# Two planner constants, the pace of sixteen scatters and the place of a layer norm's mean factor in a sparse attention layer

## The chip, the cores and the metric

The kernel runs on one core of one Trainium2 chip. Its engines are TensorE (PE, with PEld for its weight loads), VectorE (DVE), ScalarE (ACT), GpSimd (POOL) and the queue of SyncE (SP). Times are device microseconds (us) of that core; less is better.

## The reference

One layer of a graph network on 4096 nodes of width 512, with 8 heads of 64:

```python
hs = layer_norm(x);  ht = layer_norm(h_target)
q = (ht @ Wq + bq) / sqrt(64);  k = hs @ Wk + bk;  v = hs @ Wv + bv
logits = where(adj != 0, q . k per head, -1e30)
ctx = softmax(logits) @ v
ht = ht + ctx @ Wo + bo
ht = layer_norm(ht)
out = layernorm(x + ht + gelu(ht @ W1) @ W2)
```

`adj` is 4096 x 4096 and sparse: some 17 neighbours to a row, the row itself among them. All is in float32.

## The kernel before, in words

**Two programs in one.** `adj_resnorm_kernel` treats each row by the list of its neighbours. A flag tells at the end whether a list was longer than planned; only then does the dense `general_path` run, which it does not here.

**Lists.** Rows come in 32 tiles of 128. For each tile `edges` loads the adjacency rows, takes the sign on ACT (L733), and on DVE multiplies by a column count (L740) and draws the largest column numbers (L742, L749 to L766). Tiles 0 to 15 are part one, 16 to 31 are part two. `sort(part)` then ranks the rows of a part by degree on DVE and PE (L819 to L867), and POOL writes the 16 record tiles of the part to DRAM in ranked order, one indirect DMA each (L871); these are called the sort's scatters below. Part one's lists, its sort and seven of part two's tiles are done beside the projections, in the first 280 us. Nine tiles of part two and the second sort are left for the stage after.

**Attention by lists.** Ranked rows are taken in groups of two tiles (the first and the last group have one): first seven groups and a half of part one, from short lists to long, then part two from long to short. A tile has as many slots as its longest list, and slots are taken three at a time, here called a *triple*; there are 211. For a triple POOL gathers three rows of keys and values per target row into a ring of 17, later 20, slots (L985); DVE multiplies by the query (L1239), sums per head (L1244), multiplies values by the exponentials (L1200) and adds some slots (L1204, L1207); ACT takes the exponentials (L1248, L1257) and scales the third slot (L1220, L1223); PE adds up the slots by transposes into PSUM (L1211). `front` makes a tile's query: gather, scale, transposes (L1021), the product with Wq on PE (L1031) and its move out of PSUM on DVE (L1036), without which the tile's first L1239 can't start.

**After a tile.** `finish` divides (L1101 to L1122), multiplies by Wo (L1128, L1132), copies to `h` (L1137) and takes moments (L697). Once per group it then does the second layer norm: DVE shifts the variance (`n_ve`, L680), POOL raises it to the power -1/2 (`n_rs`, L687), DVE makes the mean factor (`n_nm`, L692), ACT applies both (L1150), PE transposes `h` (L1159) and ACT moves the result out as `h2T` (L1163). `finish` is advanced one step at every half group, that is twice per triple.

**Feed-forward.** `feed(g)` can start when `h2T` of group g stands. It goes in pairs: eight blocks of products with W1 (L1344) and their GELU (L1347), and, one block later, the products with W2 (L1353) into `po`. `end` then adds x (L1300), takes the sums (L1302, L1305), shifts (L1309), has POOL raise to the power (L687 again), makes the mean factor (L1314), applies both (L1317), and POOL writes the rows out (L1321). It is advanced one step with each block of the next group's feed.

**What sets the order.** `_weave` interleaves four streams by costs in the planner's own units: attention and feed are given 60 units to a group of two tiles each, the rest of the lists starts at `WAIT` units, and weights are loaded beside them. Every engine executes in order. The framework's scheduler takes the woven program, may put an instruction ahead of others whose inputs it expects later, and fixes each engine's order when the program is built. L1159, L1031, L1021, L1117, L1132 and the sort's matmuls share two PSUM buffers named `t`, so a product into `t` waits until the tile before the last one was read.

```python
            def other_lists():
                for cost in ed:
                    yield 2.2 * cost
                keep_rest()
                yield from sort(1)
            _weave((att, 0), (chain(feed(g) for g in range(len(GROUPS))), 0), (other_lists(), WAIT),
                   (weights(), 0))
```

Of the kernel before, what the change touches and what calls it, by code (L numbers as in the profile page):

```python
# [443 lines left out]
def adj_resnorm_kernel(  # L444
# [56 lines left out]
    NA, NBT = len(CAPS_A), len(CAPS_B)  # L501
# [31 lines left out]
    with tc.tile_pool(name="keep", bufs=1) as keep:  # L533
# [17 lines left out]
        with ExitStack() as late:  # L551
# [22 lines left out]
            def turn_of(name, places):  # L574
                turns[name] += 1
                return places[turns[name] % len(places)]
# [106 lines left out]
            def power(pool, mv, n, name, ve=None):  # L683
                if ve is None:
                    ve = shifted(pool, mv, n, name)
                rs = pool.tile([P, n], F32, name=name + "_rs")
                nc.gpsimd.tensor_tensor(rs, ve, mhalf[:, :n], ALU.pow)  # L687
                return rs

            def negmean(pool, mv, rs, n, name):  # L690
                nm = pool.tile([P, n], F32, name=name + "_nm")
                nc.vector.scalar_tensor_tensor(nm, mv[:, :, 0], -1.0, rs, op0=ALU.mult, op1=ALU.mult)  # L692
                return nm
# [23 lines left out]
            def behind(ins):  # L717
                return tc.issue_after(ins[-1]) if ins else nullcontext()
# [51 lines left out]
            def keep_rest():  # L770

                while held:
                    nc.sync.dma_start(*held.pop())
# [40 lines left out]
            def sort(part):  # L814

                i0, n = PARTS[part]
                me = slice(i0, i0 + n)
                pool, R = lp, Rs[part]
                nc.vector.tensor_reduce(deg[:, me], dpart[:, me, :], AX.X, ALU.add)  # L819
                nc.vector.tensor_copy(R[:, :, DEG], deg[:, me])  # L820
                dif, rank = tools[:, 928:928 + n], tools[:, 944:944 + n]
                ranki, b16 = tools[:, 960:960 + n].bitcast(I32), tools[:, 976:984].bitcast(BF16)
                nc.vector.scalar_tensor_tensor(dif, deg[:, me], float(RE), cnt[:, me], op0=ALU.min,
                                               op1=ALU.not_equal)
                nc.vector.tensor_reduce(bad[:, 1 + part:2 + part], dif, AX.X, ALU.max)
                nc.vector.tensor_scalar(dif, deg[:, me], 0.0, float(NB - 1), op0=ALU.max,
                                        op1=ALU.min)
                nc.vector.tensor_scalar(b16, dif, -1.0, float(NB - 1), op0=ALU.mult, op1=ALU.add)
                if part:
                    oh = turn_of("wide", wide).bitcast(BF16)  # L830
                else:
                    oh = wp.tile([P, NB * n], BF16, name="oh")
                oh = oh[:, :NB * n].rearrange("p (b i) -> p b i", b=NB)
                nc.vector.tensor_tensor(oh, b16.unsqueeze(1).to_broadcast([P, NB, n]),
                                        bins.unsqueeze(2).to_broadcast([P, NB, n]), ALU.is_equal)
                ohf = oh.rearrange("p b i -> p (b i)")
                pos = turn_of("wide", wide).bitcast(F32)
                pos = pos[:, :NB * n].rearrange("p (b i) -> p b i", b=NB)
                posf = pos.rearrange("p b i -> p (b i)")
                w = NB * n // 2  # L840
                yield 6.0 if part else 2.0
                tots = []
                for c in range(2):
                    sl = slice(c * w, (c + 1) * w)
                    pt = ps.tile([P, w], F32, name="t" if part else "cps", bufs=2)
                    nc.tensor.matmul(pt, ones_bf, ohf[:, sl], start=True, stop=True)
                    tots.append((sl, pt))
                if not part:
                    yield 6.0
                for c, (sl, pt) in enumerate(tots):  # L850
                    with behind([] if part else maxima):
                        scan = nc.vector.tensor_tensor_scan(
                            posf[:, sl], one_c.to_broadcast([P, w]), pt,
                            0.0 if c == 0 else posf[:, c * w - 1:c * w],
                            op0=ALU.mult, op1=ALU.add)
                while factors:
                    with behind([scan.ins]):
                        factors.pop()()
                yield 4.0
                for c in range(2):  # L860
                    sl = slice(c * w, (c + 1) * w)
                    pa = ps.tile([P, w], F32, name="t" if part else "cps", bufs=2)
                    nc.tensor.matmul(pa, lower, ohf[:, sl], start=True, stop=True)
                    nc.vector.tensor_add(posf[:, sl], pa, posf[:, sl])
                nc.vector.tensor_mul(pos, pos, oh)
                nc.vector.tensor_reduce(rank, pos.rearrange("p b i -> p i b"), AX.X, ALU.add)
                nc.vector.tensor_copy(ranki, rank)  # L867
                yield 10.0
                for i in range(n):
                    with behind(issues):  # L870
                        ins = nc.gpsimd.indirect_dma_start(  # L871
                            out=recs_d[part][:, :],
                            out_offset=bass.IndirectOffsetOnAxis(ap=ranki[:, i:i + 1], axis=0),
                            in_=R[:, i, :], in_offset=None)

                    tc.declare_no_dep(ins.ins, group=f"scatter{part}", reason="other rows")
                    tc.add_to_no_dep_group(f"scatter{part}", ins.ins)
                    yield 3.0 if part else 1.3
                done.add(part)


# [213 lines left out]
            def finish(i, p, cps, group, hs, mv):  # L1095
# [48 lines left out]
                ve = shifted(sp, mv[:, :nh, :], nh, "n2")  # L1144
                yield
                rs = power(sp, mv[:, :nh, :], nh, "n2", ve)
                yield
                nm = negmean(sp, mv[:, :nh, :], rs, nh, "n2")
                for j, h in enumerate(hs):
                    nc.scalar.activation(h, h, AF.Identity, bias=nm[:, j:j + 1], scale=rs[:, j:j + 1])  # L1150
# [144 lines left out]
            def end(group, xs, po):  # L1295

                nt = len(group)
                sm = sp.tile([P, 2, 2], F32, name="sm3")
                for j in range(nt):
                    nc.vector.scalar_tensor_tensor(xs[j], xs[j], 1.0, po[j], op0=ALU.mult,  # L1300
                                                   op1=ALU.add, accum_out=sm[:, j, 0:1])
                nc.vector.tensor_scalar_mul(sm[:, :nt, 0], sm[:, :nt, 0], -1.0 / D)  # L1302
                yield
                for j in range(nt):
                    nc.scalar.activation(po[j], xs[j], AF.Square, bias=sm[:, j, 0:1],  # L1305
                                         accum_out=sm[:, j, 1:2])
                yield
                ve = sp.tile([P, nt], F32, name="n3_ve")
                nc.vector.tensor_scalar(ve, sm[:, :nt, 1], 1.0 / D, EPS, op0=ALU.mult, op1=ALU.add)  # L1309
                yield  # L1310
                rs = power(sp, None, nt, "n3", ve)
                yield
                nm = sp.tile([P, nt], F32, name="n3_nm")
                nc.vector.tensor_mul(nm, sm[:, :nt, 0], rs)  # L1314
                yield
                for j in range(nt):
                    nc.scalar.activation(xs[j], xs[j], AF.Identity, bias=nm[:, j:j + 1],  # L1317
                                         scale=rs[:, j:j + 1])
                yield
                for j, i in enumerate(group):  # L1320
                    ins = nc.gpsimd.indirect_dma_start(  # L1321
                        out=out[:, :], out_offset=bass.IndirectOffsetOnAxis(
                            ap=tags[:, i, TGT:TGT + 1], axis=0),
                        in_=xs[j], in_offset=None)

                    tc.declare_no_dep(ins.ins, group="out", reason="other rows")
                    tc.add_to_no_dep_group("out", ins.ins)
# [68 lines left out]
            def chain(gens):  # L1396
                for g in gens:
                    yield from g

            WAIT = 100.0  # L1400
            AHEAD = 4
            ADDS = 11
            HEAVY = 30
# [68 lines left out]

            def other_lists():
                for cost in ed:
                    yield 2.2 * cost
                keep_rest()
                yield from sort(1)

            _weave((att, 0), (chain(feed(g) for g in range(len(GROUPS))), 0), (other_lists(), WAIT),
                   (weights(), 0))  # L1480

# [34 lines left out]
```

## Time and profile before

| | |
|---|---|
| three runs | 1788.15, 1792.07, 1799.92 us; median 1792.07 |
| the profiled execution | 1783.65 us, its span 1781.9 us, 22,463 instructions |
| PE busy | 1666.0 us (93%), clock granted 0.971 on average |
| DVE busy | 1425.0 us (80%) |
| ACT busy | 1240.4 us (70%) |
| POOL busy | 1018.9 us (57%) |
| first L1239 of attention | 282.3 us; last one 1656.4 us |
| last nine tiles' signs (L733) | about 383 to 708 us |
| second sort's scatters (L871) | 768 to 852 us |

The page gives busy time by engine over the whole span and in 40 slices of 44.5 us. Since stages have different limits, the waits, the stretches by window and the engines' instructions in order of time are read with it. A window's row has busy time and number of instructions for PE, PEld, DVE, ACT and POOL, then the clock that TensorE was granted, the share of the DMA engines and GB/s. A row of the waits tells who waited, for whom, the total, how often, and the longest. In a row in order of time the bracket at the end holds the idle time before it and what ended that.

### The profile page before, as it was taken

Reading aid. Unit: us, or ns where it says so; the run is one execution under the profiler, and the core shown is the slowest. Engines: PE = TensorE matmul, PEld = TensorE weight load, DVE = VectorE, ACT = ScalarE, POOL = GpSimd, SP = SyncE. Lnnn points to the kernel's source line nnn. Section 1 sums busy time; section 2 is a strip of 40 time slices with the busy share of each in tenths; the row PEclk is TensorE's granted clock in tenths of the full one; section 3 lists DMA queues with packets and bytes.
Section 4 is the critical chain, followed back from the end, with each engine's and each line's share of the span. In section 5 each row is a group of like instructions: output and inputs, shape, how many; then the busy total and the mean of one; then the engine's idle time right before and its main releaser. Section 6 shows DMA issues by size and latency. Waiting matters only on the chain. (4 is left out here: it accounts for less than half of the span.)

```text
span 1781.9 us, 22463 instructions
## 1 busy us (share of the span) xinstructions
PE 1666.0 (93%) x6850; PEld 1078.9 (61%) x6850; DVE 1425.0 (80%) x2449; ACT 1240.4 (70%) x3133; POOL 1018.9 (57%) x822
## 2 busy tenths in 40 slices
PE   7999994889999999997989999999999999999997
PEld 3444443656666776665657667666666666666665
DVE  6887787868788989996989898989897888988500
ACT  5876673648777888675777877787776777877511
POOL 1000146655557566778886787777677767764101
PEclk9999997899999999998999999999999999999998
DMA  9999988877778797867888788877667777675000
GB/s 353 383 388 367 344 272 324 318 249 270 250 241 308 273 322 268 271 204 232 285 298 284 274 282 294 295 259 260 234 218 269 249 235 239 233 260 194 21 4 26
DMA packets 141610, 461.00 MB, mean 259 GB/s; under 512 B 18036, under 2 KB 23048, under 8 KB 141480
## 3 DMA queue, kind: packets, MB, share of 16 engines
q0 software_dynamic: 96272, 342.33, 56.7%
q1 hardware_dynamic: 37392, 94.06, 14.9%
q10 hardware_dynamic: 7816, 23.08, 3.3%
q8 instruction: 57, 0.93, 0.2%
q14 instruction: 73, 0.60, 0.1%
HBM read 430.61 MB, written 28.79 MB: 258 GB/s over the span
## 5 line engine op out<-in xcount | busy, mean ns | idle before, releaser
L985 POOL DMA_INDIRECT kv<-kvd,rec x603 | 795.4, 1319 | 335.4 <-issue 118.5
L1344 PE MATMUL pf<-h2T,w 128*128 128x256 f32 (+1 forms) x2176 | 474.5, 372 | 4.5 <-ACT h2T L1163 4.5
L1353 PE MATMUL po<-w,gt 128*128 128x512 f32 x1024 | 463.7, 594 | 0.0
L1344 PEld LDWEIGHTS pf<-h2T,w 128*128 128x128 f32 x2176 | 393.0, 193 | 74.3 <-issue 20.3
L1239 DVE TENSOR_TENSOR kv<-kv,tq 128x1536 f32<-128x1536 f32 (+2 forms) x211 | 351.1, 1675 | 55.6 <-DMA kv<-kvd,rec 52.0
L1223 ACT ACTIVATE kv<-kv,pa 128x64 f32<-128x64 f32 x1520 | 390.9, 336 | 4.4
L1244 DVE TENSOR_REDUCE lg<-kv 128x24 f32<-128x1536 f32 (+2 forms) x211 | 350.0, 1667 | 0.6
L1353 PEld LDWEIGHTS po<-w,gt 128*128 128x128 f32 x1024 | 187.6, 191 | 194.5 <-issue 193.1
L1211 PEld LDWEIGHTS cps<-ident,kv 128*128 128x128 f32 x1828 | 217.6, 144 | 121.5 <-issue 41.8
L1211 PE MATMUL cps<-ident,kv 128*128 128x128 f32 x1828 | 244.1, 280 | 50.1 <-DVE kv L1200 32.1
L1200 DVE TENSOR_TENSOR kv<-kv,p 128x1024 f32<-128x1024 f32 (+1 forms) x211 | 251.1, 1192 | 25.8 <-ACT p L1248 24.4
L687 POOL TENSOR_TENSOR n_rs<-n_ve,mhalf 128x2 f32<-128x2 f32 (+2 forms) x51 | 53.4, 1047 | 327.4 <-DVE n_ve L680 133.0
L733 ACT ACTIVATE kv<-kv 128x1024 uint8<-128x1024 int32 x128 | 134.4, 1052 | 53.4 <-DMA kv<-in_adj_dram 21.8
L1347 ACT ACTIVATE gt<-pf 128x512 f32<-128x512 f32 x128 | 76.4, 597 | 100.9 <-PE pf L1344 97.4
L1347 ACT ACT_TABLE_LOAD x110 | 141.1, 1283 | 1.8
L1132 PE MATMUL t<-wo,rb 128*128 128x512 f32 x256 | 121.0, 615 | 8.1 <-DVE rb L1122 8.1
L947 PE MATMUL pq<-wv,h2T 128*128 128x512 f32 x256 | 117.0, 600 | 3.3 <-DVE rbc L662 2.4
L947 PE MATMUL pq<-wk,h2T 128*128 128x512 f32 x256 | 119.1, 608 | 1.0 <-DVE h2T L928 1.0
L1031 PE MATMUL t<-wq,tq 128*128 128x512 f32 x256 | 116.8, 600 | 1.3 <-ACT tq L1024 1.3
L742 DVE MAX8 cand<-kv 128x8 uint16<-128x171 uint16 (+1 forms) x384 | 108.2, 324 | 1.2
L1248 ACT ACTIVATE p<-lg 128x24 f32<-128x24 f32 (+2 forms) x179 | 38.9, 218 | 75.3 <-DVE lg L1244 73.9
L947 PEld LDWEIGHTS pq<-wv,h2T 128*128 128x128 f32 x256 | 48.9, 193 | 66.8 <-issue 57.5
(163 smaller groups left out, 1586.0 us busy)
## 6 DMA issues: line engine op xcount, KB each, us to landing
kv<-in_adj_dram SPq DMA_DIRECT2D x128, 512.0 KB, 7.3
kvd<-tq ACTq DMA_DIRECT2D x23, 512.0 KB, 6.9
kv<-kvd,rec POOLq DMA_INDIRECT x603, 6.0
kv<-in_L_gnn_h_target_dram SPq DMA_DIRECT2D x32, 256.0 KB, 6.3
kv<-in_x_dram SPq DMA_DIRECT2D x15, 512.0 KB, 8.5
kvd<-kv ACTq DMA_DIRECT2D x9, 512.0 KB, 6.5
w<-in_L_gnn_W_dram SPq DMA_DIRECT2D x4, 1024.0 KB, 8.2
w<-in_L_gnn_W_dram ACTq DMA_DIRECT2D x4, 1024.0 KB, 14.1
```

The source lines that it names most:

```text
L733: nc.scalar.activation(sg, a, AF.Sign, accum_out=dpart[:, i, h:h + 1])
L947: nc.tensor.matmul(pkv, hT[:, kc, j * P:(j + 1) * P], w[:, kc, :], start=kc == 0, stop=kc == KC - 1)
L985: issues[:] = [nc.gpsimd.indirect_dma_start(out=dst, out_offset=None, in_=table[:, :], in_offset=bass.IndirectOffsetOnAxis(ap=idx, axis=0) ...
L1132: nc.tensor.matmul(pa, ct[:, c, :], wo[:, c, :], start=False, stop=c == KC - 1, skip_group_check=True)
L1200: nc.vector.tensor_tensor(v4, v4, p[:, j0:j0 + m, :].unsqueeze(3) .to_broadcast([P, m, H, HD]), ALU.mult)
L1211: nc.tensor.matmul(cps[:, c, :], kv[:, j, D + c * P:D + (c + 1) * P], ident, is_transpose=True, start=j0 + j == 0 and c == 0, stop=j0 + n ...
L1223: newest[:] = [nc.scalar.mul(v, v, pa[:, hd:hd + 1]).ins]
L1239: nc.vector.tensor_tensor(kv[:, :n, :D], kv[:, :n, :D], tq[:, :D].unsqueeze(1).to_broadcast([P, n, D]), ALU.mult)
L1244: logits[:] = [nc.vector.tensor_reduce(lg[:, :n, :], kv[:, :n, :D].rearrange("p j (h d) -> p j h d", h=H), AX.X, ALU.add).ins]
L1344: nc.tensor.matmul(pf[:, k, :], w1[(f0 + k) // KC][:, kc, (f0 + k) % KC * P:((f0 + k) % KC + 1) * P], h2T[:, kc, :w], start=kc == 0, stop= ...
L1347: nc.scalar.activation(gt, pf, AF.Gelu_apprx_tanh)
L1353: nc.tensor.matmul(po[j], gt[:, k, j * P:(j + 1) * P], w2[(f0 + k) // KC][:, (f0 + k) % KC, :], start=False, stop=f0 + k == FC - 1, skip_g ...
```

## The change

Four edits. The rest of part two's lists starts at 140 planner units in place of 100, and each of its steps is given 1.6 times its cost in place of 2.2, so that the stream ends at 312.8 units in place of 337.6. The sixteen scatters of the second sort are 4.5 units apart in place of 3.0 (332.8 to 404.8 in place of 357.6 to 405.6). In `finish`, for groups that end in a tile of part two, four steps in place of one lie between POOL's power and DVE's mean factor. In `end` one more step lies between the two.

```diff
@@ sort
-                    yield 3.0 if part else 1.3
+                    yield 4.5 if part else 1.3
@@ finish
                 rs = power(sp, mv[:, :nh, :], nh, "n2", ve)
-                yield
+                for _ in range(1 if i < NA else 4):
+                    yield
                 nm = negmean(sp, mv[:, :nh, :], rs, nh, "n2")
@@ end
                 rs = power(sp, None, nt, "n3", ve)
                 yield
+                yield
                 nm = sp.tile([P, nt], F32, name="n3_nm")
@@ adj_resnorm_kernel
-            WAIT = 100.0
+            WAIT = 140.0
+            PACE = 1.6
@@ other_lists
                 for cost in ed:
-                    yield 2.2 * cost
+                    yield PACE * cost
```

## The prediction

> **What bounds the kernel now.** I read the page, the stretches by window, the waits, and then the engines in order of time around each gap of TensorE. First the page:
>
> ```profile
> span 1781.9 us, 22463 instructions
> PE 1666.0 (93%) x6850; PEld 1078.9 (61%) x6850; DVE 1425.0 (80%) x2449; ACT 1240.4 (70%) x3133; POOL 1018.9 (57%) x822
> PEclk9999997899999999998999999999999999999998
> ```
>
> PE is busy nearly throughout, at full clock save for a few slices. The stretches tell which of them have another limit (columns: PE, PEld, DVE, ACT, POOL, clock, DMA share, GB/s):
>
> ```profile
> 443.00:719.00 276.00, 271.21 (x1230) 187.44 (x1229) 234.14 (x412) 216.63 (x544) 170.34 (x137) 0.99 0.79 275
> 811.00:870.00 59.00, 46.54 (x195) 32.03 (x194) 42.70 (x44) 33.84 (x92) 47.75 (x39) 0.88 0.76 246
> 1340.00:1360.00 20.00, 15.81 (x71) 12.33 (x70) 15.48 (x22) 12.56 (x28) 12.32 (x11) 0.83 0.75 261
> 1665.00:1782.00 117.00, 104.99 (x444) 69.91 (x442) 13.13 (x75) 24.75 (x47) 11.29 (x13) 0.96 0.06 19
> ```
>
> From 443 to 719 us, where most of the lists lie, PE lacks 4.8 us in 276. After 1665 us attention is over and PE works off the feed alone. So PE's work is fixed, nothing stands behind it at the end but the last group's output, and the end moves by what PE's gaps and its slow clock cost before. The waits say who makes the gaps:
>
> ```profile
> PE cps L1211 <- DVE kv L1200: 32.1, 8, 6.6
> PE cps L1211 <- DVE kv L1204: 17.7, 9, 12.5
> PE t L1159 <- DVE tq L1036: 8.3, 2, 4.2
> DVE n_nm L692 <- POOL n_rs L687: 40.1, 27, 7.8
> ```
>
> The third and fourth row belong together. This is PE, and then DVE, at the border of two groups of part two:
>
> ```profile
> 1342.32 0.60 PE L1159 MATMUL t<-ident,h 128*128 128x128 f32 x4
> 1347.11 1.12 PE L1159 MATMUL t<-ident,h 128*128 128x128 f32 x4 [4.19 <-DVE tq L1036]
> ...
> 1348.58 5.65 PE L1344 MATMUL pf<-h2T,w 128*128 128x256 f32 x16
> ...
> 1354.28 3.62 PE L1344 MATMUL pf<-h2T,w 128*128 128x256 f32 x16
> ```
>
> ```profile
> 1339.84 0.16 DVE L692 SCALAR_TENSOR_TENSOR n_nm<-mv,n_rs 128x2 f32<-128x2 f32 x1 [7.84 <-POOL n_rs L687]
> ...
> 1344.28 0.17 DVE L1309 TENSOR_SCALAR n_ve<-sm 128x2 f32<-128x2 f32 x1 [1.58 <-ACT po L1305]
> 1346.29 0.16 DVE L1314 TENSOR_TENSOR n_nm<-sm,n_rs 128x2 f32<-128x2 f32 x1 [1.84 <-POOL n_rs L687]
> 1346.37 0.68 DVE L1036 SCALAR_TENSOR_TENSOR tq<-t,bqr 128x512 f32<-128x512 f32 x1
> ```
>
> DVE waits three times in a row, for both norms, before it reads the query out of a `t` buffer that the transposes of `h` need. PE has no feed left, idles 4.19 us, and its next 16 matmuls take 5.65 us where 3.62 is usual: the half clock after a gap.
>
> **Norm's mean factor, part two.** Four such borders cost PE. At 1067.6 us: gaps 2.65 and 0.38, then 8 matmuls in 5.29 for 3.60, in all 4.7. At 1257.8: gap 4.06, then 1.11 for 0.60 and 5.85 for 3.62, 6.8. At 1347.1: 4.19, 0.52 and 2.03, 6.7. At 1600.4: gap 2.25, then 22 matmuls in 6.32 for 4.98 and 0.37 on four transposes, 4.0. Sum 22.2 us.
>
> The Trainium skill ("TensorE: Matmul & The Clock Gate", Part 1) has the array fall to half clock after an idle window of some 3.4 us. By it the two gaps of 2.65 and 2.25 us would cost nothing more than themselves and the sum would be some 19 us; these rows show the slow matmuls after them too, and the rows stand.
>
> The order of the built programs shows what the edit really moves. L692 itself stays right behind its shift on DVE in nearly every group of part two, as before, so the 4 to 8 us that DVE waits for POOL mostly remain. What moves is the feed: `h2T` is announced three half groups later, feed starts at 612.6 units in place of 605.5 in the tenth group, and runs 7 units, one pair of blocks, behind from there. So at 1257 and 1347 PE gets two more blocks with W2 (3.44 us each) ahead of the transposes of `h`, at 1067 one, at 1600 one of each kind; and DVE's L1300 to L1314 go behind L1036 at 1257 and 1347. The filler of 6.9 us covers 4.06 and 4.19, that of 3.44 covers 2.65. I cost the delay of the feed itself at nothing: feed only slips into the 117 us at the end, where PE has no lack of it. If the filler came too early, the gaps would return whole. Taken: -22, from -26 (the 0.3 to 0.9 us gaps near them go too) to 0.
>
> **Scatters apart.** The second limit is POOL:
>
> ```profile
> 765.29 0.96 POOL L985 DMA_INDIRECT kv<-kvd,rec  x1 [2.18 <-PE cps L1211]
> ```
>
> ```profile
> 823.03 1.76 DVE L1239 TENSOR_TENSOR kv<-kv,tq 128x1536 f32<-128x1536 f32 x1 [10.63 <-DMA kv<-kvd,rec]
> ```
>
> ```profile
> 834.75 1.97 PE L1211 MATMUL cps<-ident,kv 128*128 128x128 f32 x8 [12.46 <-DVE kv L1204]
> ...
> 933.37 2.82 PE L1211 MATMUL cps<-ident,kv 128*128 128x128 f32 x12 [6.56 <-DVE kv L1200]
> ```
>
> After 765.29 POOL waits for nobody until 940.8 us; an instruction starts 0.30 us after the last ended. DVE waits 10.63 us for triple 78, and PE idles 12.46 and later 6.56. A scatter takes POOL 1.0 us and 0.3. I counted POOL's instructions in the built orders. Up to the last gather of triple 78 the changed kernel has 12 scatters and two output writes in front, before 10 and none: four more, 4 x 1.3 = 5.2 us. Against it stand the wait of 2.18 at 765, and 2.8 that POOL waited at 717 to 720 for two outputs and a rest list, which now stand 7 triples earlier. So triple 78 comes at about the same time, and **the big gap stays**. Behind it, up to triple 95, four instructions fewer: -5.2 us, which the gap at 933 (6.56, and 1.35 by 12 transposes in 2.82 for 1.47) can take. Taken: -5, from -20 (both gaps and their clock) to +6 (L687 and an output, now side by side behind triple 57, hold POOL while DVE makes both norms).
>
> **Lists later and closer.** The work is the same: per tile four L740 of 0.41 us, twelve L742 of 0.32 and some 2.6 us of decoding, about 8 us on DVE. By the two orders and the rows' means, DVE's work falls from 67.0 to 55.8 us in triples 14 to 23, and rises from 237.5 to 255.5 in triples 24 to 61. In that stretch PE's own work is 261 us, and DVE waited for PE 10.1, 6.3 and 4.7 us at L1036 of tiles 6 to 8: room for 21 of the 18 us more, but not in the same tiles. Tiles 9 to 11 have 133.9 us of DVE work (before 126.0) against 134.0 of PE, and tile 10 now ends like the border shown above, with L1300 to L1314 ahead of L1036: at most another 7. The adjacency goes along on SP's queue: 36 loads of 512 KB, 7.3 us each to landing, were 58 GB/s over the 325 us of signs and are 80 over the 236 that 172.8 units in place of 237.6 leave; at 275 GB/s and 0.79 in the window that makes some 0.85 of the DMA engines. ACT's signs move with it, to an engine busy 217 us of 276. Both at nothing, beside gathers that land before DVE asks; gathers late by it are within the upper end. Taken +5, from -3 to +18. In triples 16 to 18 the lists go away from DVE, but the order also puts L692 two triples later there: the gaps at 394 to 407 (9.0 us) become, instruction by instruction, 1.4 us longer; from -6 to +4. The sort's sums (L864) held PE 3.07 us at 752; now they stand ahead of L1036 of tile 11 with three blocks of other matmuls between. Taken -2, from -5 to +3.
>
> The skill ("SBUF — State Buffer", on the port pair that VectorE and GpSimd share) says that a two-input DVE instruction and a GpSimd one exclude each other, which speaks against closer lists. Here a gather at 811.07 took 2.16 us beside L1239 and 0.94 at 813.53 without; the L740s are as many as before and short, so no term comes of it.
>
> The extra step in `end` changes the order of L1314 by a triple at most, and is in the counts above: 0.
>
> **Sum.** -22 - 5 + 5 + 1.4 - 2 = -22.6 us on the profiled 1783.65 (span 1781.9 and 1.75 around it): 1761. The median of the runs shown is 8.4 above that execution; for the median I take 1792.07 - 22.6 = **1770**.
>
> **Rivals.**
> - *The fillers don't fill.* L692 stays where it was, and another wait ends in the same place, say ACT's h2T (L1163), for which PE waited 0.7 us after L1159 at 775. Then only -5 + 4.4 remains: 1791. For it: DVE's waits at L692 remain. Against: two blocks are 6.9 us.
> - *POOL is freed as well.* If spreading lets POOL keep its lead of some 20 us (gather's end to L1239 at triples 69 to 72), the gap of 12.46 and its slow 2.5 go too: 1770 - 15 = 1755. For it: POOL waited for ring slots up to 765. Against: the count.
> - *Slower: PE runs dry at every border.* If on the chip `h2T` really comes three half groups later in each of the nine last groups, each loses 3 x 2.8 us (102.4 us of a group over 36 half groups) less 6.9 of filler and adds one half-clock window of 1.7: 3.2 x 9 = 29, none of the 22 is won, and 1792 - 5 + 29 + 4 = 1820. It decides where L692 stands more than one triple behind L680 on DVE. The built order has it within one.
>
> **Chances.** Forecast, 1760 to 1781: 0.56. Fillers fail or the lists eat the gain, 1781 to 1800: 0.25. POOL freed, under 1760: 0.11. Slower, about 1820: 0.08. The range leaves out the last, and half of what lies beyond its other end: 1750 to 1796. Within 1% of 1792 (1774 to 1810), about what a measurement of this kernel can tell from no change, lie the second case and a third of the first's upper part: faster 0.57, same 0.35, slower 0.08.
>
> **What would show it.** L1159 after the changed borders without a wait for L1036; L1344 at 3.6 us for 16 there; L692 still waiting 4 to 8 us; POOL without waits from triple 66 on, a gap of 10 us or so at triple 78, none of 6 at triple 93; new waits of PE on L1200 near triples 50 to 58. Wrong if PE's gaps elsewhere grow: each new one of 4 us costs 6 to 7.

## The result: a little slower, and the profile after

The changed kernel takes 1797.52 us (median of 16 runs, 1790.22 to 1802.30), the kernel before 1790.47 (16 runs): a ratio of 1.0036, 95% interval 1.0021 to 1.0050, some 6.4 us more. The forecast was 22.6 us less, in a range that ended at 1796.

```profile
span 1798.9 us, 22449 instructions
PE 1669.7 (93%) x6850; PEld 1077.0 (60%) x6850; DVE 1422.3 (79%) x2449; ACT 1232.7 (69%) x3127; POOL 1010.9 (56%) x822
PEclk9999998898999999999999999999999999999999
```

The page gives DVE, ACT and POOL a few us less work than before, and PE the same matmuls in 3.7 us more. Most of the time went into PE's idle time (115.9 us of the span before, 129.2 now). The profiled execution (1800.67 us, span 1798.9) is a slow one among the 16, and that of before (1783.65) a quick one among its 16. A part of their difference has nothing to do with the change: up to the first L1239 of attention every engine has the same instructions in the same order, and this stage took 282.3 us there and 290.3 here (285.1 to 290.8 in fifteen of the sixteen profiles taken later). So I compare from that L1239 on, by stretches between the first L1239 of certain triples:

```
triples                     0-23    24-61   62-109   110-210  after 210    sum
before                     161.1    275.7    301.0     636.3     125.5   1499.6
changed                    162.1    288.6    298.5     627.4     132.0   1508.6
difference                  +1.0    +12.9     -2.5      -8.9      +6.5     +9.0
```

PE's work is the same, some 1605 us by the count of matmuls at 3.43 us for sixteen of L1344. What it idles, and what its busy time holds above that rate, is 131.3 us from the first L1239 on before and 140.9 now. By stretches of triples 0 to 23, 24 to 47, 48 to 76, 77 to 109 and from 110 on, it was 51.3, 5.9, 9.8, 29.2 and 35.1; now it is 52.5, 2.7, **30.5**, 21.8 and **33.5**. The first bold figure is the loss. The second is the gain of 22 us that did not come.

The waits tell of both (total, times, longest):

```profile
DVE n_nm L692 <- issue: 22.2, 5, 5.4
DVE n_nm L692 <- POOL n_rs L687: 20.1, 20, 4.1
PE pf L1346 <- ACT h2T L1164: 13.5, 9, 4.2
PE t L1160 <- DVE tq L1036: 1.3, 1, 1.3
```

L692 waits in total as long as before (42.3 us; 40.1 before). The wait of the transposes of `h` for L1036 fell from 8.3 us to 1.3, as forecast. But the first product of the next group (L1346, which is L1344 before) now waits 13.5 us for `h2T`, where it waited 4.5; behind triple 110 it is 9.1 for 0.4.

This is PE, and then ACT, at the border whose gap of 4.19 us the prediction showed:

```profile
1352.55 3.60 PE L1355 MATMUL po<-w,gt 128*128 128x512 f32 x8
1355.98 0.60 PE L1212 MATMUL cps<-ident,kv 128*128 128x128 f32 x4
1356.42 3.60 PE L1355 MATMUL po<-w,gt 128*128 128x512 f32 x8
1359.86 1.04 PE L1160 MATMUL t<-ident,h 128*128 128x128 f32 x8
1365.12 7.04 PE L1346 MATMUL pf<-h2T,w 128*128 128x256 f32 x18 [4.23 <-ACT h2T L1164]
```

```profile
1360.87 1.28 ACT L1258 ACT_TABLE_LOAD   x1 [8.37 <-DVE lg L1245]
...
1362.62 2.00 ACT L1224 ACTIVATE kv<-kv,pa 128x64 f32<-128x64 f32 x8
1364.53 1.90 ACT L1164 ACTIVATE h2T<-t,cols 128x256 f32<-128x256 f32 x4
```

Both blocks with W2 now stand ahead of the transposes and cover the wait for L1036. Nothing stands behind the transposes. ACT moves `h2T` out only after the exponentials and eight L1224 of two triples, and PE idles 4.23 us and runs on at half clock (18 products in 7.04 us, of which sixteen take 3.62 elsewhere), as before, one instruction later. The same happens at 1093.56 (3.50 us) and, shorter, at 1278.13 (1.13). (From L1148 on the changed kernel's lines are one to three higher than before: L1160 is L1159 there, L1212 is L1211, L1346 is L1344. Kernels with the steps of the norm alone, as norm2 below, have them one higher throughout.)

Now the stretch that lost, while DVE is at triples 47 to 51. First POOL, then DVE, then PE, in order of time:

```profile
631.58 0.58 POOL L998 DMA_DIRECT2D rec<-rec  x1 [6.03 <-DVE p L1101]
635.06 1.02 POOL L1323 DMA_INDIRECT out_dram<-xt,tags  x1 [2.89 <-ACT xt L1319]
...
652.46 1.14 POOL L985 DMA_INDIRECT xt<-in_x_dram,tags  x1 [6.21 <-DMA out_dram<-xt,tags]
```

```profile
664.96 1.76 DVE L1240 TENSOR_TENSOR kv<-kv,tq 128x1536 f32<-128x1536 f32 x1 [9.65 <-issue]
```

```profile
670.00 1.11 PE L1021 MATMUL t<-ident,tq 128*128 128x128 f32 x4 [4.76 <-ACT tq L1017]
673.34 6.05 PE L1355 MATMUL po<-w,gt 128*128 128x512 f32 x8 [2.23 <-ACT gt L1349]
```

POOL stands at a record load, at an output write, and at a gather of x whose buffer that write still reads. The gathers of keys queue behind, DVE waits 9.65 us, and PE idles 4.76 and 2.23 us, for a scaled query and for a GELU. The profile names nothing for DVE's wait here ("issue"); I take it for the gather, since in the kernel with the list edit alone the same wait is put down to it:

```profile
663.62 1.76 DVE L1239 TENSOR_TENSOR kv<-kv,tq 128x1536 f32<-128x1536 f32 x1 [8.70 <-DMA kv<-kvd,rec]
```

### The profile page after: what moved, and what is told of

The parts are those of the page before. It is cut to its first block, busy times and chain, and to the rows that moved or that the text cites. A ratio compares the mean times of both kernels' runs of the same rounds, so it can differ in the third digit from the quotient of the medians.

```text
span 1798.9 us, 22449 instructions
## 1 busy us (share of the span) xinstructions
PE 1669.7 (93%) x6850; PEld 1077.0 (60%) x6850; DVE 1422.3 (79%) x2449; ACT 1232.7 (69%) x3127; POOL 1010.9 (56%) x822
## 5 line engine op out<-in xcount | busy, mean ns | idle before, releaser
L1346 PE MATMUL pf<-h2T,w 128*128 128x256 f32 (+1 forms) x2176 | 478.7, 374 | 13.5 <-ACT h2T L1164 13.5
L1346 PEld LDWEIGHTS pf<-h2T,w 128*128 128x128 f32 x2176 | 394.6, 195 | 82.4 <-issue 19.0
L1224 ACT ACTIVATE kv<-kv,pa 128x64 f32<-128x64 f32 x1520 | 390.7, 336 | 4.1
L1212 PEld LDWEIGHTS cps<-ident,kv 128*128 128x128 f32 x1828 | 215.3, 143 | 118.0 <-issue 52.9
L1212 PE MATMUL cps<-ident,kv 128*128 128x128 f32 x1828 | 244.3, 279 | 44.8 <-DVE kv L1201 16.6
L687 POOL TENSOR_TENSOR n_rs<-n_ve,mhalf 128x2 f32<-128x2 f32 (+2 forms) x51 | 43.6, 854 | 332.3 <-DVE n_ve L680 139.0
L1132 PE MATMUL t<-wo,rb 128*128 128x512 f32 x256 | 117.4, 601 | 4.8 <-DVE rb L1122 4.8
L1031 PE MATMUL t<-wq,tq 128*128 128x512 f32 x256 | 117.3, 601 | 1.5 <-ACT tq L1024 0.9
```

The source lines that it names most:

```text
L1132: nc.tensor.matmul(pa, ct[:, c, :], wo[:, c, :], start=False, stop=c == KC - 1, skip_group_check=True)
L1212: nc.tensor.matmul(cps[:, c, :], kv[:, j, D + c * P:D + (c + 1) * P], ident, is_transpose=True, start=j0 + j == 0 and c == 0, stop=j0 + n ...
L1224: newest[:] = [nc.scalar.mul(v, v, pa[:, hd:hd + 1]).ins]
L1346: nc.tensor.matmul(pf[:, k, :], w1[(f0 + k) // KC][:, kc, (f0 + k) % KC * P:((f0 + k) % KC + 1) * P], h2T[:, kc, :w], start=kc == 0, stop= ...
```

## The experiments

All times are medians in us against the kernel before on the same chip, of 6 to 12 executions each and 21 to 33 of the kernel before. "Steps" are those between POOL's power and DVE's mean factor.

| run | edit | time | before | ratio, 95% interval |
|---|---|---|---|---|
| norm4 | before + four steps | 1802.09 | 1792.28 | 1.0055, 1.0032 to 1.0078 |
| lists | before + WAIT 140, PACE 1.6 | 1805.43 | 1792.28 | 1.0079, 1.0053 to 1.0105 |
| lists_scatter | lists + scatters 4.5 apart | 1798.99 | 1792.28 | 1.0038, 1.0018 to 1.0058 |
| endstep | before + the step in `end` | 1795.58 | 1792.28 | 1.0024, 0.9998 to 1.0050 |
| x_later | changed, x gathered two blocks later | 1803.71 | 1795.76 | 1.0033, 1.0012 to 1.0053 |
| closer | before + PACE 1.6, scatters 4.5 apart | 1802.84 | 1795.76 | 1.0044, 1.0020 to 1.0068 |
| no_norm | changed without the four steps | 1804.49 | 1795.76 | 1.0035, 1.0011 to 1.0059 |
| before_x_later | before, x gathered two blocks later | 1803.15 | 1795.76 | 1.0044, 1.0019 to 1.0070 |
| after_recs | changed + eight record buffers | 1795.84 | 1792.43 | 1.0027, 1.0006 to 1.0049 |
| after_free | after_recs + x later + first scatter later | 1801.01 | 1792.43 | 1.0057, 1.0034 to 1.0080 |
| before_recs | before + eight record buffers | 1782.80 | 1792.43 | 0.9947, 0.9926 to 0.9969 |
| norm2 | before + two steps | 1783.15 | 1792.43 | 0.9938, 0.9916 to 0.9960 |
| norm3 | before + three steps | 1785.21 | 1790.35 | 0.9974, 0.9958 to 0.9990 |
| after_norm2 | changed with two steps for four | 1787.39 | 1790.35 | 0.9984, 0.9966 to 1.0002 |
| norm2_recs | before + two steps + eight buffers | 1775.24 | 1790.35 | 0.9916, 0.9896 to 0.9936 |
| scatter2 | before, scatters 2.0 apart | 1788.65 | 1790.35 | 0.9988, 0.9971 to 1.0004 |

Each kernel has one profile. A single profile may lie several us off its kernel's median, so I rest on a stretch only where several kernels with the same edit agree in it.

### Each part alone

```diff
# norm4
-                yield
+                for _ in range(1 if i < NA else 4):
+                    yield
# lists
-            WAIT = 100.0
+            WAIT = 140.0
+            PACE = 1.6
-                    yield 2.2 * cost
+                    yield PACE * cost
# lists_scatter: lists, and
-                    yield 3.0 if part else 1.3
+                    yield 4.5 if part else 1.3
# endstep: in end, behind power
+                yield
```

The scatters could not be spread alone: 4.5 apart behind the old end of the lists, they come later than the planner needs their records.

> Only the four steps between POOL's power and DVE's mean factor in part two; lists, scatters and end as before. Theory 'lists lose' (the changed kernel's extra 7 us come from the list edit between triples 48 and 77, and the norm edit only trades PE's wait for L1036 at the borders for a wait of the next group's first W1 block for ACT's h2T): -4 to +2 us, with PE's gaps at the borders of triples 110, 141 and 154 ended by h2T, and the idle and slow time of PE after triple 110 within 5 us of the 33.5 of before. Rival 'norm loses' (feed runs 7 units late and its last 7 us come out behind attention as they are): +5 to +9 us. The prediction's term: -22 us, that idle and slow time falls to some 12 us.

> Only WAIT 140 and PACE 1.6; scatters at 3.0, norm and end as before. Theory 'lists lose': +10 to +18 us, and the idle and slow time of PE between triples 48 and 77 rises from 9.8 us to 25 to 30, with POOL standing 4 to 6 us at a gather of x that waits for an output write to land, and DVE then 8 to 10 us at an L1239. Rival 'norm loses': within 3 us of before. The prediction's term: +4 us for lists and sort sums together, up to +18 at the end of its range.

> The list edit and the scatters at 4.5 units; norm and end as before. Theory 'lists lose': 5 to 10 us less than the list edit alone, since in the changed kernel PE's idle and slow time from triple 77 to 93 was 9.4 us and before 18.2; so +3 to +10 us against before, near the changed kernel's +7. Rival 'norm loses': -8 to 0 us against before. The prediction's term: -5 for the scatters.

> Only the extra step in end. Both theories and the prediction: within 2 us of before. A third, 'end loses': the extra step puts the output write next to the gather of x on POOL, which waits for it and holds the gathers of keys behind it: +5 to +10 us, and a stop of POOL of some 6 us at a gather of x is seen here (in the built order one such place stands behind the group of triple 36, where before four gathers lie between write and gather of x) and not with the list edit alone.

**norm4** lost 9.9 us, more than either theory gave it. PE's idle and slow time behind triple 110 was 47.1 us. No gap there is ended by L1036 any more; in their place stand L1345 for `h2T` (4.06 us), L1212 for L1205 (3.42 and 3.33) and L1031 for ACT (3.73). At 1430, near triple 173, POOL's power came behind seven gathers that started after its input stood, and DVE stood still at L692:

```profile
1430.04 0.16 DVE L692 SCALAR_TENSOR_TENSOR n_nm<-mv,n_rs 128x2 f32<-128x2 f32 x1 [8.85 <-issue]
```

**lists** lost 13 to 14 us, and everything that "lists lose" said of it came: 28.9 us in triples 48 to 76, POOL 5.8 us at the gather of x, DVE 8.70 us at an L1239. **lists_scatter** gave back about 7 us by time, give or take 6. **endstep** gave no clear verdict, its interval reaching from below 0 to +9 us; POOL stood at gathers of x for 3.7, 2.3 and 5.4 us there, and one of 6 was not seen. Added up the parts would give more than 20 us, and the changed kernel has 6.4. The parts do not add.

### Is it the write, the lateness or the closeness?

```diff
# x_later (changed kernel), before_x_later (kernel before)
-                    if f0 == FC // 2:
+                    if f0 == 12:
# closer: lists_scatter with
-            WAIT = 140.0
+            WAIT = 100.0
```

> The changed kernel, with each group's gathers of x asked for at f0 = 12 in place of 8 (two blocks of W1 later), so that on POOL they no longer stand right behind the output writes whose buffer they need. Theory 'write wait' (in the list edit POOL stands 5.8 to 6.2 us at a gather of x until an output write has landed, holds the gathers of keys of triple 59 behind it, DVE idles 9 us and PE 6 to 7 and its clock falls): 8 to 11 us less than the changed kernel, 1787 to 1790; idle and slow time of PE in triples 48 to 61 from 18.5 to under 9. Rival 'close lists' (DVE's 18 us more of list work in triples 24 to 61 make attention late there, and the gather is only what DVE meets last): within 3 us of the changed kernel, 1795 to 1800, and triples 48 to 61 stay above 14.

> The kernel before with PACE 1.6 and scatters at 4.5, but WAIT 100 as before: lists closer, not later; they end at 272.8 units, 65 earlier than before. Theory 'write wait': the gathers of x stand 7 to 10 instructions behind the writes in the lists' groups here, so the stop of 6 us is gone and triples 48 to 76 stay under 18 us of idle and slow time; with scatters done sooner the gap of 12.5 us at triple 78 shrinks: -12 to -2 us against before. Rival 'close lists': DVE has more list work per triple from triple 18 to 45 than before, +5 to +15 us, idle and slow time in triples 14 to 47 above 30 us where before has 21.

> The changed kernel without the four steps of the norm (lists, scatters and the step in end stay). Theory 'parts add': 10 us less than the changed kernel, since the norm edit alone cost 9.9: 1787. Rival 'order' (what the norm edit does at each border hangs on where the built order has the neighbours, and in the changed kernel idle and slow time after triple 110 is 33.5 us, as before, though the norm edit alone has 47.1): within 3 us of the changed kernel. The prediction's term: 22 us more than the changed kernel.

> The kernel before with only the gathers of x asked for two blocks later. It measures what the write wait cost there: POOL waited 1.7 us at 540 and 4.9 at 1209 at a gather of x, with no gap of PE behind either. Theory 'write wait': within 4 us of before, either way. Rival: another place of 34 gathers moves the built order as much as any edit here did, +5 to +12 us.

**x_later** took POOL's stop of 6.2 us away (a gather of x now stands 7.3 us at 453, and PE's idle and slow time in triples 24 to 47 is 3.8 us), and with it the gap at 670, but no time. Triples 48 to 61 kept 20.3 us: PE now idled at 732, behind the sort's sums on DVE.

```profile
732.39 2.07 PE L1031 MATMUL t<-wq,tq 128*128 128x512 f32 x2 [6.72 <-DVE kv L864]
```

So the write wait was only what DVE met last, and the theory that priced it at 8 to 11 us fell. **before_x_later** showed beside this that moving those gathers costs 8 us by itself in the kernel before, which makes x_later a blunt test; after_free below repeats it, the same move included, with other holds gone. By the numbers set down beforehand, 'close lists' came in x_later (within 3 us of the changed kernel, over 14 us in triples 48 to 61).

**closer** met neither theory in full. It lost 7.9 us, as its rival said, though triples 14 to 47 had only 17.7 us of idle and slow time; triples 48 to 76 kept 27.8, and 42.8 came behind 110, where the lists are long done. Its use is in the next reading: DVE's work in triples 24 to 61, in one window each of the kernel before, the changed one, closer and after_free (the columns are those of the prediction's windows: the length, then PE, PEld, DVE and so on):

```profile
443.40:719.20 275.80, 271.01 (x1229) 187.31 (x1228) 233.91 (x412) 216.50 (x543) 170.54 (x137) 0.99 0.79 275
```

```profile
452.40:741.00 288.60, 276.74 (x1234) 189.22 (x1233) 248.48 (x473) 227.10 (x555) 166.90 (x139) 0.98 0.78 273
```

```profile
452.60:731.20 278.60, 266.99 (x1203) 185.03 (x1202) 234.36 (x402) 216.27 (x537) 174.42 (x144) 0.98 0.77 263
```

```profile
447.10:735.50 288.40, 274.95 (x1234) 188.31 (x1233) 248.72 (x474) 226.70 (x555) 167.12 (x138) 0.99 0.78 275
```

The reader is to see two pairs. With 234 us of DVE work the stretch takes 276 and 279 us, with 248.5 it takes 288 and 289. The eight other profiles without WAIT 140 have 271 to 282 us here, and the six other kernels with it, however the rest was changed, 287 to 291. DVE's idle time is 40 to 44 us in all four. Its makeup is not the same: before, 21.1 of it were waits for PE, 10.6 for gathers and 6.4 for ACT; changed, 9.4, 17.9 (the 9.65 shown above among them) and 9.6. What differs between the two groups of kernels is WAIT and with it DVE's work in the stretch; that the work is the cause is how I read the pairs, and no run adds work there by itself.

**no_norm** stands where the changed kernel does (1.0035 and 1.0036). The four steps, which lose 10 us alone, neither gain nor lose by time within the changed kernel, give or take 5 us. That is what "order" said. The two profiles are less alike than the times: behind triple 110 no_norm has some 44 us of idle and slow time where the changed kernel has 33.5, and in the stretches to triple 76 it has 6 less. One profile of each doesn't tell which of this is the edit's.

### Take POOL's holds away

```diff
# after_recs (changed kernel), before_recs (kernel before)
-                rec = sp.tile([P, E0 + MAXE], I32, name="rec", bufs=6)
+                rec = sp.tile([P, E0 + MAXE], I32, name="rec", bufs=8)
# after_free: after_recs, x_later, and ahead of the scatters
-                yield 10.0
+                yield 18.0 if part else 10.0
-                    yield 4.5 if part else 1.3
+                    yield 4.0 if part else 1.3
```

> The changed kernel with eight buffers for the records in place of six, so that POOL's load of the next record (L998) no longer waits for DVE's L1101 to have read an old one. Theory 'POOL held' (with the lists closer POOL stands 13 us at L998 between triples 48 and 62, 9 at an output write and a gather of x, and 8 at the first scatter, loses its lead of ring slots, and enters the stretch from triple 62 to 109, where its 184 instructions take 300 us whatever the scatters do, that much later): 4 to 10 us less than the changed kernel, 1788 to 1794; POOL's waits for DVE in triples 48 to 61 from 16.4 us to under 6. Rival 'next wait' (the wait only passes to the next thing, the gather of x, the scatter or DVE's own lists): within 3 us of the changed kernel, with triples 48 to 76 still above 26 us of idle and slow time.

> The changed kernel with all three holds of POOL taken away: eight record buffers, the gathers of x asked for two blocks later, and the first scatter 8 units further behind the sort, with 4.0 in place of 4.5 units between scatters, so that the last is as late as before. Theory 'POOL held': 8 to 14 us less than the changed kernel, 1784 to 1790, idle and slow time in triples 48 to 76 from 30.5 to under 18. Rival 'next wait': within 4 us of the changed kernel, and POOL or DVE wait elsewhere before triple 77.

> The kernel before with eight record buffers: POOL waited there for DVE at L998 only 1.1 us. Theory 'POOL held' and rival 'next wait': within 3 us of before. If it gains more, record buffers help by another way than the one the changed kernel shows.

"POOL held" fell; both kernels came out as 'next wait' said. In **after_recs** POOL no longer stood at L998 at 631, and the next instruction took the wait over; POOL's waits for DVE in triples 48 to 61 went from 16.4 only to 15.8:

```profile
633.80 1.02 POOL L1323 DMA_INDIRECT out_dram<-xt,tags  x1 [8.92 <-ACT xt L1319]
```

**after_free** kept 28.3 us in triples 48 to 76 and took 288.4 us for triples 24 to 61. As I read it, POOL waits because DVE, whose work the output write and the record load need in the end, is late, and the holds are followers.

**before_recs** won 9.6 us, which neither theory had. PE's and DVE's built orders are those of before, and POOL's differs in the places of a few record loads. In its profile the gaps at 1347 and 1600 have shrunk to 0.49 and 0.99 us. Why so small a move wins so much is not shown.

### How many steps

```diff
# after_norm2 (changed kernel); norm2 and norm3: the kernel before with 2 and 3
-                    for _ in range(1 if i < NA else 4):
+                    for _ in range(1 if i < NA else 2):
```

> The kernel before with two steps in place of one between POOL's power and DVE's mean factor in part two, where the norm edit has four. Theory 'delay' (each half group by which the mean factor and h2T come later costs, and four steps cost 9.9 us): +2 to +5 us. Rival 'order' (what an edit does hangs on what the built order puts next to L687 and L692, not on the size of the delay): anything from -8 to +12, and idle and slow time behind triple 110 outside 37 to 42 us. The prediction's term, by its share: -7 us.

> The kernel before with three steps between POOL's power and DVE's mean factor (two gave -9 to -11 us, four +9.9). Theory 'filler' (the blocks of W2 that feed keeps back cover PE's wait for L1036 at the borders; with each further step h2T itself comes later, and once it comes after the last block of the group before, PE waits for h2T in place of L1036): between the two, -6 to +5 us, with waits of L1345 for h2T of 2 us and more behind triple 110, fewer than with four. Rival 'order': outside of -11 to +10 us.

> The changed kernel with two steps in place of four. Theory 'parts' (lists cost 13 us, scatters and end little, and two steps win 9 behind triple 110 where four win 1.6): 6 to 10 us less than the changed kernel, -3 to +2 us against before; triples 24 to 61 as long as in the changed kernel (287 to 291 us, before 276). Rival 'order': within 4 us of the changed kernel, or above it.

One step is the kernel before. Two win 11 us, three 4.7, four lose 9.9. Neither "delay" nor the step's share of the prediction (-7) gave that; norm3's time is where "filler" put it. The shape of the row proves little by itself, since before_recs (-9.6) and before_x_later (+8) show that a new order alone moves as much. What speaks for the filler is that two steps win in three kernels: 11 us in the one before, 9.3 in the changed one and some 5.5 with eight record buffers. The time behind attention's last L1239 is 125.5 us with one step, 128.7 with two, 132.3 with three and 132.5 with four: the second and third step each keep back another 3.4 us or so of feed to fill with, the fourth hardly any more. What the fourth loses is for the most part not the wait for `h2T`, as "filler" has it: behind triple 110 that wait is 5.2 us with three and 6.1 with four, while PE's waits at L1212 for DVE's L1205 go from 1.6 to 12.1. Why is not shown. At the border of the prediction's rows, norm2 has

```profile
1344.14 1.04 PE L1212 MATMUL cps<-ident,kv 128*128 128x128 f32 x8
1345.01 1.04 PE L1160 MATMUL t<-ident,h 128*128 128x128 f32 x8
1345.88 3.60 PE L1354 MATMUL po<-w,gt 128*128 128x512 f32 x8
1349.32 0.60 PE L1212 MATMUL cps<-ident,kv 128*128 128x128 f32 x4
1349.76 3.62 PE L1345 MATMUL pf<-h2T,w 128*128 128x256 f32 x16
```

and no wait at all. One block with W2 stands **behind** the transposes and covers ACT's copy of `h2T`; in the changed kernel's rows above both stand ahead. Idle and slow time behind triple 110 is 26.0 us here against 35.1 before; with three steps 30.7, with waits for `h2T` of 2.40 and 1.97 us.

**after_norm2** is 9.3 us better than the changed kernel by their ratios to the kernel before (-2.9 and +6.4 us, whose intervals add to some 4), as 'parts' said. Where the 9 us lie is not shown: its one profile, the slowest of its 12 executions, has some 34 us of idle and slow time behind triple 110, no less than the changed kernel's. It still takes 287.9 us for triples 24 to 61, as every kernel with the closer lists.

### The scatters, and a version that beats both

> The kernel before with the second sort's scatters closer together, 2.0 units apart in place of 3.0. Theory 'POOL bound' (from triple 62 to 109 POOL's 184 instructions take some 300 us wherever the scatters stand): triples 62 to 109 take 298 to 305 us, the time is within 3 us of before. Rival, the prediction's view that the place of the scatters decides the gaps at triples 78 and 93: +4 to +10 us, with the gap at triple 78 above 15 us.

> The kernel before with two steps and eight record buffers, the two that were faster than both kernels. Theory 'parts': each won in other stretches (the buffers before triple 62 and at triple 154, the steps at 141 and 154), so -12 to -18 us against before. Rival 'order': no more than the better of the two, -8 to -11.

**scatter2** changed the step of the scatters from 3.0 to 2.0 units. The gap of PE at triple 78 grew from 12.46 to 15.96 us, as the rival said, and that at triple 93 fell from 6.56 to 4.54. The time stayed (0.9988, interval across 1). The stretch from triple 62 to 109 took 306.2 us, a us above what "POOL bound" allowed; with the scatters 4.5 apart it takes 298.5 to 300.0 us (302.8 in x_later), with 3.0 it takes 301.0 to 305.1 (309.0 in before_x_later). So their place moves the gaps within the stretch and is worth 3 to 7 us in it. That POOL bounds the stretch is not shown. It was read from POOL's rows (184 instructions in both kernels, waits of 17.7 us in 301.0 before and 9.4 in 298.5 changed). But closer gives POOL less to do there, six scatters in place of the changed kernel's fifteen and 172 instructions in all, and its stretch takes 299.0 us, with POOL waiting 21 us in it.

**norm2_recs** is faster than both kernels, 15 us less than before:

```profile
span 1772.2 us, 22462 instructions
PE 1660.3 (94%) x6850; PEld 1075.0 (61%) x6850; DVE 1423.3 (80%) x2449; ACT 1233.2 (70%) x3129; POOL 1005.5 (57%) x822
```

Its parts come to 20.7 us and it wins 15, within what 'parts' said. Triples 24 to 61 take 271.4 us as in before_recs (272.9), and 23.5 us of idle and slow time are left behind triple 110.

## Why the prediction was wrong

**The norm's mean factor: -22 forecast, about 0 measured within the changed kernel, give or take 5.** The gaps at L1036 went, and the fillers are there: 6.5 us more of feed come out behind attention. The step that failed is "the filler of 6.9 us covers 4.06 and 4.19". It counted both blocks against one wait, L1036's, and none against the next one, ACT's copy of `h2T`, which stands between the transposes and the first product: PE now waits 4.23, 3.50 and 1.13 us there at three borders. Half of the four borders were also misread. Only the gaps at 1257.8 and 1347.1 were ended by L1036; that at 1067.6 was ended by ACT's L1150 and that at 1600.4 by DVE's L1204, so 8.7 of the 22.2 us stood on other waits than the one that the argument treats. What I named as the first rival, with ACT's L1163 as the wait, is what happened; its 1791 us had the lists at +4.4. Its "against" ("two blocks are 6.9 us") was the same error: what matters is on which side of the transposes they stand. With two steps in the kernel before, the waits at both borders of L1036 are covered, and 11 us are won. That L692 stays right behind its shift and keeps waiting for POOL was right.

**Lists later and closer: +5 forecast, 13 to 14 measured alone**, inside the term's bounds (to +18). DVE's extra work in triples 24 to 61 was worked out as 18 us and is 14.6. The step that failed is "room for 21 of the 18 us more". DVE's waits for PE did fall by 11.7 us, but waits for gathers and ACT rose by 10.5, and the stretch grew by 12.9. Idle time on DVE was not room; as I read it, what DVE feeds (POOL's loads and writes, ACT's exponentials) was late in turn. That the gathers' lateness stems from the adjacency's share of the DMA engines is not borne out: the window shows 0.78 of them busy and 273 GB/s, before 0.79 and 275; I had put it at 0.85.

**Scatters apart: -5 forecast, about -7 measured** on top of the lists, give or take 6. The size fits and the detail doesn't. I expected the gap of 12.46 at triple 78 to stay and that of 6.56 at triple 93 to go. In the first one's place stand two of 5.19 and 3.29 us, at 799 (triple 71) and 852 (triple 79); the second stayed (6.45 at 951). And that POOL is the limit, on which the term rests, is what closer speaks against.

**Triples 16 to 18 and the sort's sums: +1.4 and -2.** The stretch from 0 to 23 grew by 1.0 us. L864 still stopped PE in the list kernels, by 0.57 us in the changed one for 3.07 before.

**The step in `end`: 0.** Alone +4.3 by the ratio, and not clear of zero.

**Slower.** The rival that ended on this side, PE dry at every border, is not what the changed kernel shows: it loses in the lists' stretch, not at nine borders. But norm4 alone has it in part, with POOL's power behind seven gathers and 47.1 us of lost time behind triple 110; I gave it 0.08.

## What to carry to other kernels

A filler is worth something only on the right side: list every wait between the two ends of a border, and put one block of other work behind each, not all blocks ahead of the first. Idle time of an engine that others wait for is not room for more work; ask who waits for what it does next. When several small shifts are made in an order that a scheduler fixes, measure each alone, in several sizes, and together: here two steps win about what four lose, and the parts do not add.

## What was not expected of the hardware

The length of a gap does not tell whether PE is slow behind it. The prediction's gap of 2.25 us in the kernel before, at 1600.4, was followed by slow matmuls. In norm2 one of the same length is not: fourteen products take 3.19 us, as many as at full clock. In norm3 one of 2.76 us is: eight products in 5.37 us that take 3.60 elsewhere.

```profile
1621.13 0.66 PE L1212 MATMUL cps<-ident,kv 128*128 128x128 f32 x4 [2.27 <-DVE kv L1208]
1621.62 3.19 PE L1345 MATMUL pf<-h2T,w 128*128 128x256 f32 x14
```

```profile
1071.90 5.37 PE L1354 MATMUL po<-w,gt 128*128 128x512 f32 x8 [2.76 <-ACT gt L1348]
```

The first fence is norm2, the second norm3, both PE in order of time. What decides can be read from the granted clock. In all eighteen traces it is either full or half, its half stretches start a whole number of steps of 3.41 us apart, and each lasts one such step or several. Here are the step with the gap and the one after it, for the kernel before, norm3 and norm2 (length; busy time of PE, PEld, DVE, ACT, POOL; clock; share of the DMA engines; GB/s):

```profile
1598.28:1601.69 3.41, 1.24 (x11) 1.16 (x12) 3.41 (x7) 3.20 (x13) 0.93 (x1) 1.00 0.05 22
1601.69:1605.11 3.42, 3.42 (x11) 2.85 (x11) 3.42 (x5) 3.42 (x12) 2.90 (x2) 0.50 0.67 177
```

```profile
1068.46:1071.88 3.42, 0.68 (x7) 0.44 (x5) 3.42 (x5) 3.29 (x9) 2.81 (x3) 1.00 0.73 247
1071.88:1075.29 3.41, 3.39 (x4) 1.50 (x5) 3.41 (x3) 3.39 (x7) 2.80 (x3) 0.50 0.67 250
```

```profile
1616.96:1620.38 3.42, 1.90 (x6) 0.76 (x4) 2.34 (x3) 2.03 (x10) 1.02 (x2) 1.00 0.78 274
1620.38:1623.79 3.41, 2.66 (x15) 2.41 (x16) 3.41 (x6) 3.39 (x9) 2.13 (x2) 1.00 0.30 61
```

The first two gaps lie almost wholly within one step and leave PE busy for 1.24 and 0.68 us of it; the next step is at half clock. Norm2's gap of 2.27 us lies across the end of a step, which leaves 1.90 and 2.66 us, and the clock stays. It is so in all eighteen traces from attention's first L1239 on: of the steps at full clock, all 196 with PE busy, by the profile, under 0.40 of the step were followed by half clock, none of the 7159 with more than 0.51, and 23 of the 82 between. PE need not be idle for a whole step, then, and a gap of 2.2 to 2.8 us may or may not cost some 1.7 us besides itself (half of a step), by where it falls. The slow time in the tables above holds this luck: behind triple 110 PE idled 16.0 us in the kernel before and 11.8 in norm2, but the clock was at half for 20.5 and 6.8.

And the stage before attention, with the same instructions in the same order, took between 281.9 and 290.8 us from one profile to another. That is more than most of the differences measured here, and a reason to compare stretches and not spans.
